# Four graph-attention layers on one core: the first unit's copies on VectorE, two additions of layer 3 by accumulating DMAs, elu's constants by GpSimd, and a new order of the work

## The chip, the core and the metric

The kernel runs on one core of a Trainium2 chip. A core has five engines with a queue each: TensorE (PE: matmuls, and PEld for its weight loads), VectorE (DVE), ScalarE (ACT), GpSimd (POOL) and SyncE (SP, which only issues DMAs here). Each works its own queue in order and waits there for semaphores. The metric is the time of one execution on the device in microseconds.

## The reference

Eight batches (B = 8) of 2048 nodes with 128 features go through four layers; all share one adjacency matrix of 2048 x 2048. Every layer is `x = x + layer(relu(layernorm(x)))`.

- Layers 0, 1 and 3 are graph attention with one head: `Wh = h W`, scores `leaky_relu(f1[i] + f2[j])`, masked by the adjacency, softmax over j, times `Wh`. Layer 0 ends with elu. Layer 3 scales its input per node, normalises `Wh` (gamma, beta), adds it again to the result, and ends with elu.
- Layer 2 is attention with four heads of 32 features, whose scores are the products of h with itself.

elu(a) is computed as `relu(a) + min(exp(a), 1) - 1`.

Cut to the end of layers 0 and 3:

```python
h_prime = jnp.einsum('bij,bjd->bid', attention, Wh)
return jax.nn.elu(h_prime)                    # layer 0
h_prime = jnp.einsum('bij,bjo->bio', attention, h) + residual
return jax.nn.elu(h_prime)                    # layer 3
```

## The kernel before, in words

**Units.** One batch in one layer is a unit, written (batch, layer) with layers 0, 1, 2, 3. `X[b]` is the batch's x, 128 partitions x 2048 columns, which stays in SBUF from its load (line 420) to the store of its two halves (line 880).

**Start of a unit.** `Unit.rows_made` normalises x: statistics on VectorE (line 451), a power on GpSimd (line 111, out `rstdx`), then the rows `h` on ScalarE (line 511), four blocks of 128 nodes per quarter. TensorE transposes a quarter (line 540). In a one-head layer (`Gat`) ScalarE copies the transposes to SBUF (`h_t`, line 558), TensorE multiplies by the weights (line 566), and `put` takes exponentials of the scores (lines 595 to 597) and writes the scaled rows `y` (line 591), all on ScalarE. `spread` makes `r`, the target's factor in all 128 partitions: for (0, 0), (0, 1) and (7, 3) by TensorE transposes (line 650) and a ScalarE copy (line 659), for others through DRAM.

**Tokens.** The attention of a one-head unit is 32 tokens: two halves of the targets times 16 blocks of sources. A token is one VectorE instruction, the front (line 718: factors `r`, `cr` and the mask `edge` into `zg`), and eight matmuls of 128 x 129 (line 727, two records each in the profile). Three `zg` buffers lie between them. There are 24 units with 32 tokens, 768 in all.

**Beats.** A unit of layer 2 is 64 beats, 512 in all. A beat is two score pairs on TensorE (line 994, two matmuls each), two exponentials on ScalarE (line 1001, 128 x 1024 each), one mask on VectorE (line 1007, 128 x 2048), and a weighing on TensorE (line 1016, four matmuls of 32 rows for one beat, mostly two beats at a time). Five `z` buffers lie between them. After 16 beats `finish` copies, transposes, divides and adds to x by an accumulating DMA from GpSimd's queue (line 1041).

**End of a half.** `out` divides the sums on VectorE into `oa` (line 760; one buffer). Layer 1 adds `oa` to x by an accumulating DMA of GpSimd (line 795). Layer 0 takes `exp` into `oe` and `relu` into `oa` on ScalarE (line 766), adds `min(oe, 1)` to x on VectorE (line 789) and `oa` by the DMA; its -1 is left out there, since layer normalisation does not see a constant. Layer 3 adds the residual `oe` (line 781), multiplies by gamma (line 783), adds beta (line 785), then `exp` and `relu`, and on VectorE line 789 and line 792, which adds `oa` and the -2 for both elus. `DIRECT` names units whose additions stay on VectorE.

**Start of the program.** SyncE issues the loads of x and of 16 adjacency rows of 1 MB (line 366); VectorE converts each to `edge` (line 369). TensorE also tests that the adjacency is symmetric (lines 382 and 386), with squares on ScalarE (line 392).

**Order.** Nothing here is ordered by hand alone. `Plan` is a planner that runs at build time: every piece of work is an `Op` with an engine, a duration, a due time, what it needs, which buffers it takes and frees, and a lag until others can see its result. `Plan.run` places at each step the op that can start first; among those that can start within `WINDOW_US` on an engine it takes the one with the earliest due time, lowered by `HURRY_US` for fronts while `zg` has more than one free buffer. The due times come from the tables `EARLY`, `TOKENS`, `BEATS` and `LEADS`. The result is a fixed order on each queue.

## Time and profile before

| | us |
|---|---|
| Median of 3 runs | 2755.65 |
| Lowest and highest | 2753.89, 2758.16 |
| Profiled execution, own time | 2748.61 |
| Its span, first to last instruction | 2746.8 |
| TensorE busy, as modelled | 2626.4 |
| VectorE busy | 2515.0 |
| ScalarE busy | 1720.2 |
| GpSimd busy | 261.7 |

A busy time is the sum over an engine's instructions; those of TensorE end where a model says so. In a list of groups, each line gives the line of the kernel, the engine, the operation, what it writes and reads, the count, the busy time, the mean duration in ns, and the idle time of the engine just before those instructions with what ended it. In a timeline a line gives start, length, engine, line and operands; brackets hold the idle time before it and what ended it.

### The profile page before, as it was taken

The page shows a single profiled execution, that of the slowest core. Times are in us where ns is not written, and L with a number is a line of the kernel's source. Part 1 is how long each engine was busy: PE and PEld are TensorE (multiplying, and loading weights), DVE is VectorE, ACT ScalarE, POOL GpSimd, SP SyncE. Part 2 cuts the span into 40 slices and gives each one's busy share as a digit, 9 for nine tenths or more (in the row PEclk, how much of TensorE's full clock was granted, in tenths as well). Part 3 has the DMA queues.
Part 4 walks back from the last instruction along what each step waited for, and adds up shares of the span by engine and source line. Part 5 has one row for each costly group of instructions (what it writes and reads, how often), then busy time and mean ns, then how long its engine had stood idle before and what let it go on. Part 6 is the DMA issues. An engine that isn't in the chain of part 4 may idle for free. (4 is left out here: it accounts for less than half of the span.)

```text
span 2746.8 us, 48941 instructions
## 1 busy us (share of the span) xinstructions
PE 2626.4 (96%) x20104; PEld 2020.1 (74%) x20104; DVE 2515.0 (92%) x3323; ACT 1720.2 (63%) x2789; POOL 261.7 (10%) x114
## 2 busy tenths in 40 slices
PE   6999999989998999999999999999999999999987
PEld 6999877757774777867777677786787667565677
DVE  7868899989999899999999999999999899899987
ACT  4333665576567558666767666665676757787651
POOL 2101010011000101111100110010111100011000
PEclk9999999999999999999999999999999999999999
DMA  8003223433323223232323321423225221422000
GB/s 311 17 9 99 64 55 62 93 85 62 62 47 77 55 55 85 55 70 55 67 62 81 78 47 47 103 53 70 55 59 105 47 58 28 108 54 55 13 16 25
DMA packets 212842, 181.80 MB, mean 66 GB/s; under 512 B 142448, under 2 KB 177728, under 8 KB 206464
## 3 DMA queue, kind: packets, MB, share of 16 engines
q1 hardware_dynamic: 144112, 156.46, 21.1%
q0 software_dynamic: 68080, 22.04, 8.0%
q8 instruction: 160, 2.62, 0.4%
q14 instruction: 74, 0.61, 0.1%
q10 hardware_dynamic: 416, 0.07, 0.0%
HBM read 123.03 MB, written 33.73 MB: 57 GB/s over the span
## 5 line engine op out<-in xcount | busy, mean ns | idle before, releaser
L1001 ACT ACTIVATE z<-ps,shift 128x1024 f32<-128x1024 f32 x1024 | 1122.7, 1113 | 727.1 <-PE ps L994 721.4
L727 PEld LDWEIGHTS ps<-y,zg 128*128 128x128 f32 x12288 | 1466.0, 192 | 71.3 <-DVE zg L718 20.0
L727 PE MATMUL ps<-y,zg 128*128 128x129 f32 x12288 | 1497.1, 276 | 15.5 <-DVE zg L718 10.4
L1007 DVE SCALAR_TENSOR_TENSOR z<-z,edge 128x2048 f32<-128x2048 f32 x512 | 1169.3, 2285 | 64.0 <-ACT z L1001 63.2
L718 DVE SCALAR_TENSOR_TENSOR zg<-r,cr,edge 128x1024 f32<-128x1024 f32 x768 | 970.5, 1278 | 98.1 <-PE ps L727 88.0
L994 PE MATMUL ps<-m,s 128*128 128x512 f32 x2048 | 721.1, 438 | 63.6 <-ACT z L1001 59.1
L994 PEld LDWEIGHTS ps<-m,s 128*128 128x128 f32 x2048 | 314.2, 191 | 339.4 <-ACT z L1001 241.1
L1016 PE MATMUL ps<-z,v 128*32 128x512 f32 x4096 | 500.9, 601 | 2.2 <-DVE z L1007 1.6
L1016 PEld LDWEIGHTS ps<-z,v 128*32 128x32 f32 x4096 | 103.5, 109 | 234.4 <-issue 183.3
L511 ACT ACTIVATE h<-x,nmrx,rstdx 128x128 f32<-128x128 f32 x512 | 210.7, 491 | 32.7 <-DVE nmrx L116 18.6
L111 POOL TENSOR_TENSOR rstdx<-varx,neg_half 128x16 f32<-128x16 f32 x31 | 130.3, 4204 | 643.9 <-DVE varx L106 643.9
L1041 POOL DMA_DIRECT2D x<-o x31 | 65.8, 2124 | 906.8 <-DVE o L1036 811.8
L451 DVE BATCH_NORM_STATS2 st<-x 128x6 f32<-128x128 f32 x496 | 106.2, 278 | 0.0
L566 PEld LDWEIGHTS ps<-rhs,h_t 128*128 128x128 f32 x768 | 98.3, 194 | 10.7 <-ACT h_t L558 3.0
L566 PE MATMUL ps<-rhs,h_t 128*128 128x130 f32 x768 | 104.3, 281 | 0.4 <-ACT h_t L558 0.3
L540 PE MATMUL ps<-ident,h 128*128 128x128 f32 x512 | 79.9, 279 | 15.7 <-ACT h L511 10.9
L795 POOL DMA_DIRECT2D x<-oa x26 | 23.4, 901 | 702.3 <-ACT z L1001 189.3
L540 PEld LDWEIGHTS ps<-ident,h 128*128 128x128 f32 x512 | 62.1, 142 | 35.0 <-ACT h L511 13.9
L760 DVE TENSOR_TENSOR oa<-ps,rs 128x384 f32<-128x384 f32 x144 | 73.9, 513 | 5.0
L558 ACT COPY h_t<-ps 128x512 f32<-128x512 f32 x96 | 55.2, 581 | 34.9 <-PE ps L540 34.9
L766 ACT ACTIVATE oe<-oa 128x1024 f32<-128x1024 f32 x32 | 33.8, 1058 | 68.8 <-DVE oa L785 59.2
L591 ACT ACTIVATE y<-ps,y 128x128 f32<-128x128 f32 x256 | 73.0, 369 | 0.0
(123 smaller groups left out, 830.7 us busy)
## 6 DMA issues: line engine op xcount, KB each, us to landing
s<-halves SPq DMA_DIRECT2D x256, 128.0 KB, 2.7
m<-halves SPq DMA_DIRECT2D x64, 512.0 KB, 6.5
r<-row SPq DMA_DIRECT2D x42, 512.0 KB, 3.7
raw<-in_adj_dram SPq DMA_DIRECT2D x16, 1024.0 KB, 16.9
x<-oa POOLq DMA_DIRECT2D x26, 512.0 KB, 4.6
values<-h SPq DMA_DIRECT2D x32, 256.0 KB, 2.2
halves<-hi SPq DMA_DIRECT2D x128, 64.0 KB, 1.7
halves<-lo SPq DMA_DIRECT2D x128, 64.0 KB, 1.7
```

The source lines that it names most:

```text
L111: nc.gpsimd.tensor_tensor(out=rstd, in0=v, in1=neg_half, op=OP.pow)
L451: nc.vector.bn_stats(out=key["st"][:, n, :], in_=rows()[:, n, :])
L511: nc.scalar.activation(self.h[q][:, k, :], X[self.b][:, n, :], AF.Relu, scale=key["rstd"][:, n:n + 1], bias=key["nmr"][:, n:n + 1])
L540: nc.tensor.transpose(pk[:, k, :], self.h[q][:, k, :], ident)
L566: nc.tensor.matmul(pv[:, k, :C + 2], lhsT=self.h_t[q][:, k * P:(k + 1) * P], rhs=rhs, start=True, stop=True)
L718: nc.vector.scalar_tensor_tensor(z, self.r[half], self.cr[:, 0, jb:jb + 1], edge[:, jb, half * HN:(half + 1) * HN], op0=OP.max, op1=OP.mult)
L727: nc.tensor.matmul(ps[:, self.banks(half, place)[i // 3], k * CE:(k + 1) * CE], lhsT=z[:, i * P:(i + 1) * P], rhs=self.y[:, jb, :], start= ...
L760: nc.vector.tensor_mul(key["a"][:, i0:i1, :], pv[:, :, :C], r[:, i0:i1, None].to_broadcast([P, i1 - i0, C]))
L994: nc.tensor.matmul(ps[:, lo + c, :], lhsT=self.S[h, jb // HB][:, at:at + P], rhs=self.M[h][:, (c2 * 2 + c) * 512:(c2 * 2 + c + 1) * 512], ...
L1001: nc.scalar.activation(self.z[s][:, c2 * HN:(c2 + 1) * HN], ps[:, lo:lo + 2, :].rearrange("p b t -> p (b t)"), AF.Exp, bias=shift)
L1007: nc.vector.scalar_tensor_tensor(self.z[s], self.z[s], 1.0, edge[:, jb, :], op0=OP.mult, op1=OP.mult, accum_out=self.den[:, h, jb:jb + 1])
L1016: nc.tensor.matmul(ps[c * HD:(c + 1) * HD, 0, :], lhsT=self.V[h][:, jb, :], rhs=z[:, c * 512:(c + 1) * 512], start=jb == 0, stop=jb == NB - 1,
```

## The change

Five things change in the code, and the planner then gives every queue a new order.

1. **First unit, (0, 0).** The four copies to `h_t` and the sixteen scaled copies to `y` (four wide multiplications now) run on VectorE. The exponentials stay on ScalarE. Fronts and the transposes of `r` need only the exponentials (`r_made`), and the first half's transposes take the PSUM bank of the sums.
2. **Layer 3, batches 0 to 6.** The addition of the residual (`L3_DMA`) and that of `oa` to x (`L3_PLUS`) become accumulating DMAs from GpSimd's queue. Batch 7 keeps both on VectorE.
3. **The constants of elu.** GpSimd subtracts 2 from x, 128 x 2048, once per batch: after the load for batches 1 to 7, for batch 0 once its first rows are made.
4. **Loads of x** for batches 1 and later wait until all adjacency rows are in. The second target tile of (0, 2) is taken through a one-element copy on GpSimd. Three small kinds of statistics buffers are now counted by the planner.
5. **The planner's numbers.** Durations, lags and all tables of due times are new.

```diff
-    HURRY_US, WINDOW_US, BEAT_SUMS_US = 70.8, 0.139, 0.86
+    HURRY_US, WINDOW_US, BEAT_SUMS_US = 38.6, 0.138, 0.86
-    EARLY = dict(front=-107.6, score=111.1, exp=-8.6, mask=-164.7, sums=-334.5)
+    EARLY = dict(front=-419.0, score=436.6, exp=-72.7, mask=-319.1, sums=-351.0)
-    DIRECT, ROWS_TURNED, L1_ACT, L3_DMA, L3_OUT = ((0, 0), (0, 1), (7, 1), (7, 2)), True, False, False, False
+    DIRECT, ROWS_TURNED, L1_ACT, L3_DMA, L3_OUT = ((0, 0), (0, 1), (7, 1), (7, 2)), True, False, True, False
+    L3_PLUS, LESS_US = True, 3.0
...
-            x_taken[b] = add("SP", 2.0, due, load, takes=["x"], lag=17.0 if b else 4.5)
+            x_taken[b] = add("SP", 0.8 if b else 2.8, due, load, loaded[:] if b else (), takes=["x"], lag=17.0 if b else 3.5)
             done[b, 0] = [x_taken[b]]
+            if b:
+                done[b, 0] = [less_two(b, due, done[b, 0])]
+
+        def less_two(b, due, needs):
+            return add("POOL", LESS_US, due + 18.0, lambda op: nc.gpsimd.tensor_scalar(
+                X[b], X[b], -2.0, None, op0=OP.add), needs)
...
+                self.less = [less_two(0, 60.0, [m[1] for m in made])] if (self.b, layer) == (0, 0) else []
...
+                    begins = (self.b, layer) == (0, 0)
...
-                        nc.scalar.copy(self.h_t[q], ps[:, turn.got["pair"], :])
+                        (nc.vector.tensor_copy if begins else nc.scalar.copy)(self.h_t[q], ps[:, turn.got["pair"], :])
...
+                    if begins:
+                        exped.append(add("ACT", 0.45, self.due(part + 0.04), lambda op, q=q, product=product:
+                                         self.put(q, product.got["pair"], False), [product] + exped[-1:]))
+                        ends.append(add("DVE", 0.75, self.due(part + 0.05), lambda op, q=q, product=product:
+                                        self.put_on_vector(q, product.got["pair"]), [exped[-1]],
+                                        frees=[("pair", product)]))
+                        continue
...
+            def put_on_vector(self, q, lo):
+                pv = ps[:, lo:lo + 2, :].rearrange("p b (k c) -> p (b k) c", c=256)
+                sl = slice(q * 4, q * 4 + 4)
+                nc.vector.tensor_mul(self.y[:, sl, :C], pv[:, :, :C], self.y[:, sl, C:CE].to_broadcast([P, 4, C]))
...
+                        room = "sums" if (self.b, self.layer, half) == (0, 0, 0) else "pair"
...
                 def elu_a(op):
-                    nc.vector.scalar_tensor_tensor(xs(), key["a"], -2.0, xs(), op0=OP.add, op1=OP.add)
+                    nc.vector.scalar_tensor_tensor(xs(), key["a"], 0.0, xs(), op0=OP.add, op1=OP.add)
...
-                last = add("DVE", 1.14, late + 4, elu_a, [last, e], frees=[("oa", taker)])
+                if L3_PLUS and b != B - 1:
+                    last = add("POOL", PLUS_US, late + 4, plus_a, [last, e], frees=[("oa", taker)], lag=PLUS_LAG_US)
+                else:
+                    last = add("DVE", 1.14, late + 4, elu_a, [last, e], frees=[("oa", taker)])
...
+                if (self.b, h) == (0, 1):
+                    def hold(op):
+                        self.M[h] = big.tile([P, N], F32R, tag="m", name="m")
+                        nc.gpsimd.tensor_copy(self.M[h][0:1, 0:1], self.M[0].bitcast(F32)[0:1, 0:1])
+                    held = add("POOL", 1.0, due, hold, self.first_target, takes=["m"])
+                    self.there, there, m_taken = there + [held], there + [held], []
...
         TOKENS = {
-            (1, 0, 0): (-22.6, 16.91), (0, 1, 0): (53.7, 14.45), (0, 1, 1): (278.3, 12.5),
+            (1, 0, 0): (-1045.4, 4.85), (0, 1, 0): (-640.7, 2.76), (0, 1, 1): (-252.6, 5.26),
...
         BEATS = {
-            (0, 0): (-186.75, 13.08), (0, 1): (-165.33, 21.31), (0, 2): (148.16, 8.98),
+            (0, 0): (-220.15, 3.75), (0, 1): (-955.77, 16.21), (0, 2): (-787.01, 14.33),
...
         LEADS = {
-            (0, 0): 491.95, (1, 0): 357.11, (0, 1): 1280.8, (2, 0): 1208.77, (1, 1): 234.77,
+            (0, 0): 213.98, (1, 0): 444.85, (0, 1): 1602.72, (2, 0): 431.88, (1, 1): 877.58,
...
```

## The prediction

> **What bounds the kernel now.** I read the page first, then the time in six windows cut at work that both versions share, then the timeline where TensorE's price per piece of work can be read, last the chain at the end.
>
> ```profile
> span 2746.8 us, 48941 instructions
> PE 2626.4 (96%) x20104; PEld 2020.1 (74%) x20104; DVE 2515.0 (92%) x3323; ACT 1720.2 (63%) x2789; POOL 261.7 (10%) x114
> ...
> L1001 ACT ACTIVATE z<-ps,shift 128x1024 f32<-128x1024 f32 x1024 | 1122.7, 1113 | 727.1 <-PE ps L994 721.4
> ...
> L1007 DVE SCALAR_TENSOR_TENSOR z<-z,edge 128x2048 f32<-128x2048 f32 x512 | 1169.3, 2285 | 64.0 <-ACT z L1001 63.2
> L718 DVE SCALAR_TENSOR_TENSOR zg<-r,cr,edge 128x1024 f32<-128x1024 f32 x768 | 970.5, 1278 | 98.1 <-PE ps L727 88.0
> ```
>
> TensorE and VectorE are both nearly full, and neither can run far ahead of the other. The busy share of TensorE is modelled, so I price its work by the distance from one start to the next:
>
> ```profile
> 2601.57 1.06 PE L1016 MATMUL ps<-z,v 128*32 128x512 f32 x8
> 2602.56 0.73 PE L994 MATMUL ps<-m,s 128*128 128x512 f32 x2
> ...
> 2604.79 1.95 PE L727 MATMUL ps<-y,zg 128*128 128x129 f32 x16
> 2606.49 0.70 PE L994 MATMUL ps<-m,s 128*128 128x512 f32 x2
> 2607.03 1.95 PE L727 MATMUL ps<-y,zg 128*128 128x129 f32 x16
> ```
>
> Token and score pair take 2607.03 - 2604.79 = 2.24 us; tokens in a row stand 1.79 apart, so a token is 1.79 and a pair 0.45 to 0.46. A weighing is 0.85 per beat plus 0.31 for each turn into the narrow form (pair and weighing, 2600.94 to 2602.56, are 1.62 = 0.46 + 0.85 + 0.31). Transposes are 0.11, projections 0.22, a symmetry matmul 0.055 per 128 columns. For the whole kernel: 768 x 1.79 + 1024 x 0.46 + 512 x 0.85 + 287 x 0.31 + 709 x 0.11 + 384 x 0.22 + about 18 = 2550 us.
>
> ```profile
> 0.00:36.00 36.00, 15.77 (x74) 11.43 (x75) 22.07 (x75) 18.98 (x60) 15.71 (x19) 1.00 0.93 365
> 36.00:88.50 52.50, 51.06 (x438) 49.59 (x439) 46.72 (x96) 15.90 (x59) 3.53 (x2) 0.97 0.45 158
> 88.50:186.70 98.20, 97.73 (x888) 93.30 (x886) 68.61 (x96) 44.09 (x127) 7.89 (x3) 1.00 0.06 17
> 186.70:2619.90 2433.20, 2360.97 (x17873) 1766.77 (x17872) 2280.35 (x2917) 1599.50 (x2448) 227.88 (x89) 1.00 0.30 64
> 2619.90:2732.10 112.20, 100.87 (x837) 98.96 (x836) 90.25 (x137) 39.60 (x96) 6.73 (x2) 0.94 0.05 15
> 2732.10:2746.80 14.70, 0.00 (x0) 0.00 (x0) 6.99 (x8) 2.11 (x2) 0.00 (x0) 0.65 0.14 41
> ```
>
> Columns: window, length, busy time of PE, PEld, DVE, ACT, POOL, granted clock, DMA share, GB/s. Stage I ends after the 64th token (186.7): 150.2 us of priced work, 36.5 idle. Stage II ends with the last weighing (2619.9): 2305.9 of work, 127.3 idle. Stage III ends with the last matmul: 93.4 of work, 18.8 idle. The tail has 14.7 us with no matmul. A change of order can only win from these 197 us.
>
> **The change, part by part.** The changed program was counted in the order in which it issues instructions on each engine. TensorE's work is the same: 2549.9, with 288 turns for 287.
>
> *Stage I.* The load of batch 1 no longer stands ahead of batch 0's: 1 MB at 365 GB/s is 2.8 us, so x and each adjacency row come that much earlier. Four copies (0.58) and sixteen scaled copies (1.14 per quarter) leave ScalarE's chain for VectorE, and the first row of r needs two quarters instead of waiting behind all four. Before, that copy ran at 33.50 and the first front at 34.52. Adding the same rows in the new order (half of x at 7.6; statistics, 1.7 of power and its end 11.6; twelve rows of h at 0.40 to 16.4; second exponentials 19.0; transposes 0.9; copy 1.0) gives r at about 21. Six edge conversions and the new copies stand before the first front in VectorE's queue, and the sixth row lands at 27.7 - 2.8 = 25, so the front comes at 26.7, 8 us earlier. Ten pairs of conversion and front follow at the pace of the rows, 2.6 us; before token 11 there is 30.4 us of TensorE work (31.5 before; symmetry now fills these gaps), and it comes at about 54 instead of 63.6: idle 24 instead of 32. Then a block of 52 statistics with their moments, 10 us without a front, stands before front 23, against two tokens in hand: 3.6 idle. GpSimd subtracts 2 from four batches here: I charge 3. Stage I: 24 + 3.6 + 3 = 31 idle, 5.5 won.
>
> *Stage II.* Fourteen additions of `oe` (1.14 apart) and fourteen of `a` go from VectorE to DMAs; in this stage 25 wide ones fewer, 28 us, and 8 fronts fewer (10 us), with 7 tokens fewer for TensorE (12 us, done in stage III). VectorE falls from about 2290 (2280 busy in the window) to 2252, TensorE from 2305.9 to 2293.7. What that is worth depends on how the work is mixed: beats need 2.2 us on VectorE and ScalarE but 1.8 to 2.1 on TensorE, tokens 1.2 against 1.79. So I took both orders four beats at a time, and summed the excess of the fullest engine over TensorE: 133 us before (the trace has 127), 115 after. Eight at a time: 78 and 71. Scaled to 127, that is 110 and 117; I take 113. In it is one bad stretch: beats 400 to 416 now have no tokens, 47 us of TensorE work against 73 of ScalarE's (32 exponentials and the rows of three units): 24 us idle at one place.
>
> The 28 extra DMAs cost 0.90 us of GpSimd each, which is 90% idle, and land 4.5 to 9.4 us after issue, median 4.6. The multiplication by gamma waits for the first one; behind it in VectorE's queue are fronts and masks. Between divide and multiplication the new order holds 4.6 to 12 us of other VectorE work, so the wait is 0 at the median and 21 us over fourteen at 9.4. I take 0, the median's value. `oa` is held longer, but the next divide is 24 us or more away, beyond what two landings (9.2) add to the usual 10 to 16.
>
> The subtraction (x, 128x2048) has no row. Least is VectorE's conversion of the same shape, 1.25; most is GpSimd's select, 0.32 for 128 columns, times 16 = 5.1. I take 3.6, the select less the 0.10 that a one-column memset takes, because engine and kind are its own. The load is hundreds of us early, so only a hold of VectorE matters. The nearest row is the power:
>
> ```profile
> 370.52 1.28 DVE L718 SCALAR_TENSOR_TENSOR zg<-r,cr,edge 128x1024 f32<-128x1024 f32 x1
> 370.75 3.84 POOL L111 TENSOR_TENSOR rstdx<-varx,neg_half 128x16 f32<-128x16 f32 x1 [1.40 <-DVE varx L106]
> ...
> 371.71 2.31 DVE L1007 SCALAR_TENSOR_TENSOR z<-z,edge 128x2048 f32<-128x2048 f32 x1
> ```
>
> The power takes 2.89 when no front runs; here it takes 3.84, as if it began when the front ended (371.80). The mask beside it loses 0.02. Ends per pass: 0.02 and 5.1. As the power reads 16 columns and then computes, I stay away from the low end, but up to three made fronts (5.4 us of TensorE work) cover a hold: 1 us per pass, 3 in stage I as said and 5 in stage II. Stage II: 113 + 5 = 118 idle, 9 won.
>
> The Trainium skill, page "SBUF — State Buffer", section "Who interferes with whom", speaks against this: a VectorE instruction with two SBUF inputs and a GpSimd one that reads SBUF lock the same port pair for a whole instruction, and the second waits. The trace shows only GpSimd as the loser. By the rule all eight passes would hold VectorE throughout, 29 us at 3.6 each, and the sum would end 21 us later.
>
> *Stage III.* From the last mask to the first token of (7, 3) the chain is 52 us long. Before, 16 tokens fill it, and five wide operations of batch 6 stand among the statistics:
>
> ```profile
> 2629.61 2.97 PE L727 MATMUL ps<-y,zg 128*128 128x129 f32 x16 [2.98 <-DVE zg L718]
> ...
> 2635.29 8.25 PE L727 MATMUL ps<-y,zg 128*128 128x129 f32 x48 [2.70 <-DVE zg L718]
> ```
>
> After, 23 tokens are left for it (41 us, with weighing and projections 49), and fronts stand among the statistics. Its idle time falls to 2, and the 4 us among the last 32 tokens stay: 6 instead of 18.8, 13 won. The tail is batch 7's, which keeps all its VectorE operations: 14.7.
>
> **The sum.** 5.5 + 9 + 13 = 27.5, so a span of 2719.3. The profiled execution took 2748.61 and the median is 2755.65, 7.0 above, so 2728.
>
> **Rivals.** *The stretch without tokens is not bought back.* Its 24 us come on top of an unchanged 127, because the page puts most of the idle on waits for exponentials, not for additions: 24 - 18.5 = 5.5 later, 2761; it is slower from 18.5 us at that place on. Against it: the count outside the stretch falls by a third. *GpSimd holds VectorE.* 5.1 us at all eight passes, all reaching TensorE: 41 - 8 = 33 on the sum, 2761; it decides from 4.4 us per pass. *The freed VectorE time counts in full.* 38 us off stage II's idle instead of 9: 2699. For it: both engines are within 1% there. *Only the end wins,* if stage I stays at the pace of the rows and stage II is as before: 2743.
>
> **How the numbers follow.** Forecast 0.50 (own range 2708 to 2740), only the end 0.16, full count 0.12, stretch 0.14, GpSimd 0.08. About 0.2% (5.5 us) is what can be told from no change. Both slower rivals lie at that bound: of their 0.22 I put 0.16 beyond and 0.06 within; of the end's 0.16, 0.03 is within. Faster 0.75, same 0.09, slower 0.16. The range from 2700 to 2763 takes in the 21 us of landings as well, and leaves out about 2 in 10.
>
> **What would show it.** First front near 27 us and the 64th token done near 181; no additions of lines 781 and 792 on VectorE before batch 7; a hole of some 24 us around beat 400; less than 4 us of TensorE waits between last weighing and first token of (7, 3); masks that stay at 2.29 us beside the subtraction. The prediction is wrong if stage II's idle is not between 95 and 140, or if multiplications by gamma wait for DMAs.

## The result, and the profile after

The changed kernel takes 2758.28 us (median of 20 executions, 2754.17 to 2765.24), the kernel before 2753.09 in the same comparison (20 executions, 2747.79 to 2760.15). The ratio is 1.0021, 95% interval 1.0014 to 1.0029: 5.2 us slower, where 27.5 us less were forecast. The profiled execution of the changed kernel took 2765.24 us, the longest of its 20; that of the kernel before took 2748.61, near the shortest of its 20. Their difference of 16.6 us overstates the change by 11, so sizes are taken from medians below, and places from the traces.

From the page of the changed kernel (part 1 and the costliest groups; the last column is the idle time before these instructions and what ended it):

```profile
span 2763.5 us, 49024 instructions
PE 2637.1 (95%) x20104; PEld 2024.9 (73%) x20104; DVE 2515.8 (91%) x3303; ACT 1712.1 (62%) x2769; POOL 331.5 (12%) x151
...
L765 PE MATMUL ps<-y,zg 128*128 128x129 f32 x12288 | 1499.2, 277 | 30.5 <-DVE zg L756 22.2
L1064 DVE SCALAR_TENSOR_TENSOR z<-z,edge 128x2048 f32<-128x2048 f32 x512 | 1170.3, 2287 | 70.4 <-ACT z L1058 67.8
L756 DVE SCALAR_TENSOR_TENSOR zg<-r,cr,edge 128x1024 f32<-128x1024 f32 x768 | 992.8, 1309 | 113.5 <-PE ps L765 97.2
```

VectorE lost 28 wide additions and is as busy as before (2515.8 against 2515.0). Part of it is in the fronts, which do the same work in 992.8 us instead of 970.5: 1309 ns on average for 1278. TensorE waits for fronts 22.2 us instead of 10.4. The timeline shows where, beside the second to eighth of GpSimd's eight passes. Here is the fifth (start, length, engine, line; "x2" is two in a row):

```profile
862.14 5.89 POOL L431 TENSOR_SCALAR x<-x 128x2048 f32<-128x2048 f32 x1 [12.77 <-DMA x<-in_x_dram]
...
862.72 5.86 DVE L756 SCALAR_TENSOR_TENSOR zg<-r,cr,edge 128x1024 f32<-128x1024 f32 x2
...
867.44 0.82 PE L765 MATMUL ps<-y,zg 128*128 128x129 f32 x5 [1.69 <-DVE zg L756]
```

Two fronts take 5.86 us there. The first has 4.67 in the trace, 3.39 more than its usual 1.28. The other passes beside fronts look the same, but for the sixth, where the front takes 3.87. At the first pass it is an edge conversion, which otherwise takes 1.23:

```profile
17.55 5.37 POOL L431 TENSOR_SCALAR x<-x 128x2048 f32<-128x2048 f32 x1 [5.17 <-DMA raw<-in_adj_dram]
17.70 6.31 DVE L371 TENSOR_SCALAR edge<-raw 128x2048 uint8<-128x2048 int32 x1
```

The excess of all VectorE instructions beside the eight passes, over their usual durations, is 28 us. The seven passes beside fronts share a pattern. Each starts while a VectorE instruction still runs and ends 5.2 us after that one's end, so first GpSimd waits and then VectorE. The held front ends 0.65 us before its pass does. Four statistics of VectorE, which read one SBUF input each, run beside the sixth pass in their usual 0.28 us; the front behind them comes later, and so is held for less (2.6 us).

The same stages as in the prediction (end of the 64th token, of the last weighing, of the last matmul; columns as there: window, length, busy time of PE, PEld, DVE, ACT, POOL, granted clock, which is the recorded share of TensorE's full clock, DMA share, GB/s):

```profile
0.00:199.70 199.70, 171.03 (x1396) 160.81 (x1396) 157.33 (x272) 73.07 (x224) 50.24 (x27) 0.95 0.32 116
199.70:2630.60 2430.90, 2354.96 (x17762) 1754.47 (x17760) 2256.11 (x2882) 1595.31 (x2440) 269.24 (x117) 1.00 0.33 69
2630.60:2748.60 118.00, 111.04 (x952) 109.62 (x948) 95.29 (x144) 41.63 (x104) 12.05 (x7) 0.97 0.18 42
2748.60:2763.50 14.90, 0.10 (x1) 0.00 (x0) 7.09 (x8) 2.11 (x2) 0.00 (x0) 0.66 0.13 40
```

With TensorE's work priced as in the prediction (150.2, 2293.7 and 106.0 us), the idle time is:

| | before | predicted | after | after, passes cut to one column |
|---|---|---|---|---|
| Stage I | 36.5 | 31 | 49.5 | 40.2 |
| Stage II | 127.3 | 118 | 137.2 | 119.7 |
| Stage III | 18.8 | 6 | 12.0 | 12.1 |
| Tail | 14.7 | 14.7 | 14.9 | 14.8 |

The last column is the first experiment below.

### The profile page after: what moved, and what is told of

Read it like the earlier page. It is cut to its first block, busy times and chain, and to the rows that moved or that the text cites. A ratio compares the mean times of both kernels' runs of the same rounds, so it can differ in the third digit from the quotient of the medians.

```text
span 2763.5 us, 49024 instructions
## 1 busy us (share of the span) xinstructions
PE 2637.1 (95%) x20104; PEld 2024.9 (73%) x20104; DVE 2515.8 (91%) x3303; ACT 1712.1 (62%) x2769; POOL 331.5 (12%) x151
## 5 line engine op out<-in xcount | busy, mean ns | idle before, releaser
L765 PE MATMUL ps<-y,zg 128*128 128x129 f32 x12288 | 1499.2, 277 | 30.5 <-DVE zg L756 22.2
L756 DVE SCALAR_TENSOR_TENSOR zg<-r,cr,edge 128x1024 f32<-128x1024 f32 x768 | 992.8, 1309 | 113.5 <-PE ps L765 97.2
L834 POOL DMA_DIRECT2D x<-oa x40 | 35.7, 892 | 934.5 <-DVE oa L798 239.6
L460 DVE BATCH_NORM_STATS2 st<-x 128x6 f32<-128x128 f32 x496 | 106.0, 282 | 1.1 <-DMA x<-oa 1.1
```

What stands on the lines that cost most here:

```text
L460: nc.vector.bn_stats(out=key["st"][:, n, :], in_=rows()[:, n, :])
L756: nc.vector.scalar_tensor_tensor(z, self.r[half], self.cr[:, 0, jb:jb + 1], edge[:, jb, half * HN:(half + 1) * HN], op0=OP.max, op1=OP.mult)
L765: nc.tensor.matmul(ps[:, self.banks(half, place)[i // 3], k * CE:(k + 1) * CE], lhsT=z[:, i * P:(i + 1) * P], rhs=self.y[:, jb, :], start= ...
```

## The experiments

Each kernel ran on one chip beside the kernel before, whose median there was 2752.1 to 2753.9 us. The table gives medians, and the ratio to the kernel before with its 95% interval. The groups of experiments ran on different chips, and differences between kernels of different groups are of medians; by the ratios, the 19.7 us below would be 18.4.

| kernel | made from | us | ratio |
|---|---|---|---|
| passes cut to one column | changed | 2738.5 | 0.9954 (0.9942 to 0.9967) |
| the first four cut | changed | 2751.2 | 0.9994 (0.9985 to 1.0002) |
| passes in sixteen pieces | changed | 2749.8 | 0.9987 (0.9977 to 0.9996) |
| subtraction by DMA | changed | 2738.4 | 0.9952 (0.9939 to 0.9965) |
| additions back on VectorE | changed | 2776.6 | 1.0087 (1.0074 to 1.0100) |
| additions by DMA, old order | before | 2788.0 | 1.0129 (1.0112 to 1.0147) |
| the same, no DMA for -2 | before | 2770.2 | 1.0059 (1.0043 to 1.0074) |
| copies back on ScalarE | subtraction by DMA | 2739.2 | 0.9951 (0.9937 to 0.9964) |
| batch 1's x early | subtraction by DMA | 2739.9 | 0.9945 (0.9932 to 0.9957) |
| the same, TensorE busier | batch 1's x early | 2736.3 | 0.9942 (0.9930 to 0.9955) |
| wide rows in the stretch | subtraction by DMA | 2740.3 | 0.9949 (0.9936 to 0.9961) |
| wide rows elsewhere | subtraction by DMA | 2740.4 | 0.9951 (0.9939 to 0.9964) |
| *on one chip:* subtraction by DMA | changed | 2742.0 | 0.9962 (0.9949 to 0.9976) |
| batch 1's x early | subtraction by DMA | 2738.8 | 0.9951 (0.9936 to 0.9965) |
| the same, TensorE busier | batch 1's x early | 2735.0 | 0.9936 (0.9922 to 0.9951) |
| the same at three places | batch 1's x early | 2734.6 | 0.9933 (0.9917 to 0.9949) |

My theory after the traces was that the passes hold VectorE and that the hold reaches the end of the program. The rivals were that other work covers it, and that the new order, with its long stretch without tokens, is what costs.

### The passes, all eight and the first four

```diff
-            return add("POOL", LESS_US, due + 18.0, lambda op: nc.gpsimd.tensor_scalar(
-                X[b], X[b], -2.0, None, op0=OP.add), needs)
+            return add("POOL", LESS_US, due + 18.0, lambda op: nc.gpsimd.tensor_scalar(
+                X[b][:, 0, 0:1], X[b][:, 0, 0:1], 0.0, None, op0=OP.add), needs)
```

The second kernel has this for batches 0 to 3 alone.

> The eight GpSimd passes over x are cut to one column each, with a constant of 0, and every instruction keeps its place; elu's constant of -2 is left out of batches' sums. Theory A (a pass holds VectorE for as long as it works, and VectorE has no slack where the first four passes lie): the wide fronts beside a pass go back from 4.66 to 1.28 us, the first front comes at about 26.7 instead of 32.2 us, the 64th token ends 13 us earlier than 199.7 (5.5 from the first pass, 7 to 8 from the next three), and each of the four late passes gives 0 to 3.4 us: 2740 to 2748 in all, about 12 to 20 below the changed kernel, so faster than the kernel before by 0.3 to 0.6%. Theory B (the passes are paid for by slack; only the first front moves): 3 to 6 us below the changed kernel, 2752 to 2755, no difference to the kernel before. Theory C (nothing hangs on the passes, the stretch without tokens is the whole cost): 2758.

> Only the passes of batches 0 to 3 are cut to one column (a constant of 0 in place of -2, which these batches' outputs then lack); those of batches 4 to 7 are whole. Theory A: first front at 26.7, 64th token some 13 us earlier than 199.7, and 11 to 14 us below the changed kernel in all (2744 to 2747). If it gains as much as the kernel with all eight cut, the four late passes cost nothing; if the difference is over 5 us, they cost as much as their hold. Theory B: 3 to 6 us. Theory C: nothing.

Measured: 2738.5 with all eight cut, 19.7 below the changed kernel; 2751.2 with the first four cut, 7.0 below. The four late passes are thus worth 12.7 us, which is what their four holds sum to in the trace (three of 3.4, one of 2.6). I had not thought that any hold would come through so completely where three fronts may be made ahead. The first four are worth 7.0, of 15.2 us of holds. No front is longer than 1.29 us in the first of these kernels. Stages of its trace:

```profile
0.00:190.40 190.40, 164.31 (x1396) 153.82 (x1396) 143.01 (x272) 73.34 (x224) 29.00 (x27) 0.98 0.33 121
190.40:2603.80 2413.40, 2347.76 (x17762) 1753.42 (x17761) 2242.86 (x2882) 1594.93 (x2440) 249.65 (x117) 1.00 0.33 70
2603.80:2721.90 118.10, 111.11 (x952) 109.61 (x948) 95.48 (x144) 41.62 (x104) 12.05 (x7) 0.97 0.18 41
```

Theory A holds, theories B and C fall. Some numbers of A missed: the first kernel is just below its 2740 to 2748 and the second above its 2744 to 2747, the first front comes at 29.4 and not at 26.7 us, and the 64th token ends 9.3 us earlier and not 13. So the early passes cost less than I expected there, and something else keeps stage I longer than before (190.4 against 186.7).

### The passes in pieces

```diff
-            return add("POOL", LESS_US, due + 18.0, lambda op: nc.gpsimd.tensor_scalar(
-                X[b], X[b], -2.0, None, op0=OP.add), needs)
+            def subtract(op):
+                for n in range(NB):
+                    nc.gpsimd.tensor_scalar(X[b][:, n, :], X[b][:, n, :], -2.0, None, op0=OP.add)
+            return add("POOL", LESS_US, due + 18.0, subtract, needs)
```

> The changed kernel, with each of the eight GpSimd passes over x (128x2048) as sixteen instructions of 128 columns in its place; same result, same order. Theory M (what holds VectorE is one GpSimd instruction at a time): a wide front beside the pieces waits for one or two of them, 1.3 to 2.0 us each in place of 4.66, the pass takes longer (6 to 12 us, as it now waits for fronts in turn), and 8 to 16 of the 19.7 us come back that the kernel with one-column passes gained: 2742 to 2750. Rival N (what counts is the total time that GpSimd works in SBUF, however it is cut): the fronts beside it lose as much in sum, 2755 to 2762.

2749.8, 8.5 below the changed kernel: theory M, at the upper end of its range. In the trace the roles are turned round at the same place (here GpSimd's line joins eight pieces):

```profile
859.47 11.32 POOL L433 TENSOR_SCALAR x<-x 128x128 f32<-128x128 f32 x8 [12.49 <-DMA x<-in_x_dram]
...
860.33 2.53 DVE L759 SCALAR_TENSOR_TENSOR zg<-r,cr,edge 128x1024 f32<-128x1024 f32 x2
862.79 2.37 DVE L1067 SCALAR_TENSOR_TENSOR z<-z,edge 128x2048 f32<-128x2048 f32 x1
```

Two fronts take 2.53 us, a mask 2.37 instead of 2.29, and the excess of all VectorE instructions beside the pieces is about 2 us in place of 28. GpSimd pays: a piece takes 0.53 us at the median and 0.97 on average, since four in ten are held up, most by a front or a mask, and a pass takes 11 to 24 us instead of 5.4 to 6.2. The three passes of batches 1 to 3 cost most: they run from 55.0 to 88.4 us, the statistics of these batches wait behind them, and the 64th token ends at 197.3, nearly as late as in the changed kernel (199.7). Stage II takes 2418.7 us, 5.3 more than with the passes cut; its trace has seven windows of half clock there against three, and whether the late pieces cost anything beside these is not shown.

The Trainium skill, page "SBUF — State Buffer", section "Who interferes with whom", states that a VectorE instruction with two SBUF inputs contends with a GpSimd instruction that reads SBUF, the shared port pair being an exclusive lock. Of VectorE's two-port modes it says that whoever issues first has the pair "for the whole instruction; the other **fully blocks** (not throttle)". The prediction weighed the rule and chose the other side. The runs agree with it on who waits, with 28 us lost beside long passes and about 2 beside short pieces. They do not show the hold to last for a whole pass: a front that ends 0.65 us before the pass and needs 1.28 was free to begin 1.9 us before the pass's recorded end.

### The subtraction by DMA

```diff
+        def constants():
+            nc.gpsimd.memset(twos, -2.0)
+            nc.scalar.dma_start(out=minus_2, in_=twos)
...
+            def subtract(op):
+                if 0 < b < B - 1:
+                    for half in range(2):
+                        nc.gpsimd.dma_start(out=X[b][:, half * HB:(half + 1) * HB, :], in_=minus_2, accum_op=OP.add)
...
-                    nc.vector.scalar_tensor_tensor(xs(), key["a"], 0.0, xs(), op0=OP.add, op1=OP.add)
+                    nc.vector.scalar_tensor_tensor(xs(), key["a"], -2.0 if b == B - 1 else 0.0, xs(), op0=OP.add, op1=OP.add)
```

Batch 0's -2 is the scalar of its own addition in layer 0.

> The whole computation, without a pass of GpSimd over x: batches 1 to 6 get their -2 by two accumulating DMAs of 512 KB from a tile of -2 in DRAM, batch 0's is the scalar of its own addition, batch 7's stays in elu on VectorE. Theory A: as with the passes cut to one column, give or take 2 us for the 6 MB of DMA in 12 transfers and some 1 us of GpSimd for each: 2740 to 2750, faster than the kernel before by 0.1 to 0.5%; the fronts beside the old places of the passes take 1.28 us. Theory C: 2758, or more if the DMAs delay other transfers.

2738.4, the same as with the passes cut, and just below the range of theory A. The whole work of the changed kernel, with the constants taken through DMAs, is 0.48% faster than the kernel before.

### The additions put back

```diff
-                    nc.gpsimd.dma_start(out=xs(), in_=key["a"], accum_op=OP.add)
+                    if layer == 3:
+                        nc.vector.tensor_add(xs(), xs(), key["a"])
+                    else:
+                        nc.gpsimd.dma_start(out=xs(), in_=key["a"], accum_op=OP.add)
...
-                        last = add("POOL", PLUS_US, due + 6, lambda op: nc.gpsimd.dma_start(
-                            out=key["a"], in_=key["e"], accum_op=OP.add), [last] + rows, lag=PLUS_LAG_US)
+                        last = add("POOL", PLUS_US, due + 6, lambda op: nc.vector.tensor_add(
+                            key["a"], key["a"], key["e"]), [last] + rows, lag=PLUS_LAG_US)
```

> Layer 3's 28 additions (14 halves, two each) that the change gave to accumulating DMAs are VectorE's again, at the same place in the order, 1.12 us each; the passes stay. If VectorE bounds and the time freed counted in full: 31 us above the changed kernel, about 2789. If it counts as my sum had it (part of the stretches bound by VectorE, part covered): 10 to 18 above, 2768 to 2776. If it lay beside other work everywhere: 0 to 3 above, 2758 to 2761, and if the transfers were late where they are used, below 2758.

2776.6, 18.3 above the changed kernel: 0.65 us for each, with 1.12 us of VectorE for an addition. That is just above the 10 to 18 of the middle theory, which my sum had used. It is not the full count, and it is not covered.

### The additions alone, in the old order

Taking them away from the kernel before should then have won as much, if the order does not matter:

```diff
-                    if k == 0:
+                    if k == 0 and b != B - 1:
+                        nc.gpsimd.dma_start(out=a, in_=key["e"], accum_op=OP.add)
+                    elif k == 0:
...
                 def elu_a(op):
+                    if b != B - 1:
+                        nc.gpsimd.dma_start(out=xs(), in_=key["a"], accum_op=OP.add)
+                        return
```

> The kernel before, in its own order, with one part of the change alone: layer 3's 28 wide additions by accumulating DMAs, each at its old place in the order. The constant -2 that one of them carried is added by two DMAs of 512 KB from a tile in DRAM ahead of layer 0's sum (batches 1 to 6) and by the scalar of an addition that is there anyway (batch 0); batch 7 is as before. No copy is moved, no pass of GpSimd, no new dues. Theory F (the freed VectorE time is worth 0.65 us per us, as putting it back cost 18.3 us for 28 additions, and it needs no new order): 2733 to 2738, 15 to 20 below the kernel before. Theory G (it is worth that only in an order planned for it; in the old one the DMAs come later than VectorE's sums did and the units behind them start late): 2748 to 2756, no difference.

2788.0, 36 us slower than the kernel before, outside all that I had expected. VectorE's statistics waited 18.2 us for x behind my own extra DMAs, so a second kernel leaves those out:

> As the kernel before with layer 3's 28 additions by DMA in the old order, but without the DMAs that add -2 ahead of layer 0's sum: the constant -2 is left out of batches 0 to 6. If the 18.2 us that VectorE's statistics waited there for x were the fault of those extra DMAs: 2762 to 2772, some 16 to 26 below that run's 2788.0, and still above the kernel before, since VectorE's multiplications by gamma wait 20 to 25 us for the first of the two DMAs. Theory F as stated there (a gain of 15 to 20 in any order) would need 2733 to 2738; theory G's no difference 2748 to 2756.

2770.2, still 16 above the kernel before. Its waits on VectorE (line waiting, what for; us in total, times, longest):

```profile
DVE zg L718 <- PE ps L727: 90.4, 130, 3.4
DVE z L1012 <- ACT z L1006: 77.2, 125, 2.8
DVE oa L785 <- DMA oa<-oe: 23.6, 7, 6.8
```

The old order has the multiplication by gamma too close behind the addition; VectorE stands in front of it until the DMA has landed. Its masks also wait longer for exponentials (77.2 us; 63.2 in the kernel before). This trace is of the shortest execution, 2761.2. In the changed kernel's order the same wait is:

```profile
DVE oa L821 <- DMA oa<-oe: 3.2, 2, 2.4
```

So theory F falls: the additions by DMA win in the new order, which leaves room for the landing, and lose in the old one, which does not. That the waits for the landing are the whole of the loss is not shown: 23.6 us of waits, less the 18.3 that the additions are worth in the new order, would make 5.3 and not 16.

### The first unit's copies

In the kernel with the subtraction by DMA, the copies of `h_t` and the scaling of `y` are ScalarE's again, each in its place:

```diff
-                        (nc.vector.tensor_copy if begins else nc.scalar.copy)(self.h_t[q], ps[:, turn.got["pair"], :])
+                        nc.scalar.copy(self.h_t[q], ps[:, turn.got["pair"], :])
...
-                nc.vector.tensor_mul(self.y[:, sl, :C], pv[:, :, :C], self.y[:, sl, C:CE].to_broadcast([P, 4, C]))
+                for k in range(4):
+                    n = q * 4 + k
+                    nc.scalar.activation(self.y[:, n, :C], pv[:, k, :C], AF.Copy, scale=self.y[:, n, C:CE])
```

> The kernel with the subtraction by DMA, with the first unit's four copies of h_t and its sixteen scalings of y on ScalarE again (each at its own place in the order; VectorE has 5.4 us less, ScalarE 8 us more). As my sum had it (every us of the first front counts): the first front comes 3 to 8 us later than 30.0 and the time is 3 to 8 us above 2738.4. Theory D: the second unit's tokens come at 124.3 whatever the first unit does, so the gap of 16.0 us in front of the 33rd front takes up the delay: the first front 3 to 8 us later, the 64th token within 1 us of 192.4, the time 2737 to 2740.

2739.2, no difference; the first front comes at 30.2 instead of 30.0 and the 64th token ends at 192.2 instead of 192.4. Both expectations were wrong on the first front: who does the copies does not set it. VectorE now stands idle for the sixth adjacency row, which must be converted ahead of the first front:

```profile
28.73 1.23 DVE L371 TENSOR_SCALAR edge<-raw 128x2048 uint8<-128x2048 int32 x1 [1.23 <-DMA raw<-in_adj_dram]
...
30.20 1.28 DVE L769 SCALAR_TENSOR_TENSOR zg<-r,cr,edge 128x1024 f32<-128x1024 f32 x1
```

The gap of theory D had nothing to take up, so this run neither supports nor harms that theory.

### The second unit's x

What keeps stage I long without the passes is visible between the 32nd and 33rd front. In the kernel with the subtraction by DMA:

```profile
108.31 1.28 DVE L767 SCALAR_TENSOR_TENSOR zg<-r,cr,edge 128x1024 f32<-128x1024 f32 x1
...
120.43 3.19 DVE L471 BATCH_NORM_STATS2 st<-x 128x6 f32<-128x128 f32 x16
...
124.33 1.28 DVE L767 SCALAR_TENSOR_TENSOR zg<-r,cr,edge 128x1024 f32<-128x1024 f32 x1
```

16.0 us without a front; the kernel before has 2.3 there. The change loads batch 1's x behind all sixteen adjacency rows. One line lets it go behind twelve:

```diff
-            x_taken[b] = add("SP", 0.8 if b else 2.8, due, load, loaded[:] if b else (), takes=["x"], lag=17.0 if b else 3.5)
+            x_taken[b] = add("SP", 0.8 if b else 2.8, due, load, loaded[:12 if b == 1 else NB] if b else (), takes=["x"], lag=17.0 if b else 3.5)
```

> The kernel with the subtraction by DMA, and batch 1's load of x waits for 12 of the 16 adjacency loads in place of all 16 (the planner then puts the first layer of batch 1 earlier, and shifts the rest). Theory D (stage I is longer than before because the second unit cannot begin: its x lands behind the whole adjacency, and the 33rd front follows the 32nd after 16.0 us, at 124.3 us, where before it followed after 2.3): that gap falls under 7 us, the 64th token ends at 181 to 185 in place of 192.4, and the whole at 2727 to 2732, 7 to 11 below 2738.4. Theory E (stage I is bound by VectorE's statistics and by the squares of the symmetry test, which stay): the gap moves but the 64th token ends at 190 to 192 and the time stays within 2 us of 2738.4.

The gap falls to 6.3 us and the 64th token ends at 184.9, 7.5 earlier, as theory D had it. But the time is 2739.9: nothing arrives at the end. Behind stage I the order of the two kernels is the same, and the trace of this one loses 11 us on the way, near 565 and 1217 us and in and behind the stretch without tokens. At each of these places the record of the granted clock has windows of 3.4 us at half of full speed: ten between the 64th token and the last weighing, against one in the kernel that it was made from.

### The stretch without tokens

From 2102.79 to 2215.92 us the changed kernel has no front, 113 us and 31 beats; the longest such stretch before is 47 us.

```profile
2102.79 1.28 DVE L756 SCALAR_TENSOR_TENSOR zg<-r,cr,edge 128x1024 f32<-128x1024 f32 x1
...
2215.92 1.28 DVE L756 SCALAR_TENSOR_TENSOR zg<-r,cr,edge 128x1024 f32<-128x1024 f32 x1 [4.75 <-DMA r<-row]
```

First, is ScalarE its bound, as the prediction said? Two kernels merge ScalarE's small instructions there, and elsewhere:

```diff
+                    if merged():
+                        n = q * 4
+                        nc.scalar.activation(self.h[q], X[self.b][:, n:n + 4, :], AF.Relu,
+                                             scale=key["rstd"][:, n:n + 1], bias=key["nmr"][:, n:n + 1])
+                        return
                     for k in range(4):
```

> The kernel with the subtraction by DMA. In the 31 beats without tokens (388 to 418 of 512), groups of four 128-column ScalarE instructions that prepare a unit (rows of h, node weights, scaling of y) are one instruction of 512 columns; the scale and bias of the second to fourth row blocks of each group are left out. 16 groups: ScalarE does some 15 us less there. Theory H (the stretch is bound by ScalarE, and nothing later gives the time back): 11 to 16 us below 2738.4, 2722 to 2727. If TensorE's 18.7 us of idle there are not ScalarE's, or the stages after it wait for something else: within 3 us of 2738.4.

> The same edit at beats 270 to 300, where tokens run beside the beats: 20 groups of four, some 18 us less work for ScalarE (the scale and bias of the second to fourth row blocks of each group are left out). Theory H: ScalarE bounds nothing there, 2735 to 2739. If ScalarE's work counts wherever it lies: some 15 to 18 us below 2738.4.

2740.3 and 2740.4, no gain in either place, so theory H falls. ScalarE has 9.2 us less to do in the stretch (94.35 busy, then 85.20; the wide instructions took 0.7 to 0.8 us and not the 0.6 I had assumed), and the stretch is 1.9 us shorter. Most of the rest went into waits for scores, first in the kernel with the subtraction by DMA, then in this one:

```profile
ACT z L1072 <- PE ps L1065: 13.7, 10, 2.9
```

```profile
ACT z L1086 <- PE ps L1078: 18.0, 16, 1.8
```

Second, does the clock matter there? In the kernel with batch 1's x early, TensorE gets more to do, of which nothing is used:

```diff
+                if 392 <= self.b * HEADS * NB + s <= 416:
+                    nc.tensor.matmul(ps[:, 2, :256], lhsT=self.S[h, jb // HB][:, at:at + P],
+                                     rhs=self.M[h][:, :256], start=True, stop=True)
```

> The kernel with batch 1's x early, and in beats 392 to 416 of the stretch without tokens TensorE does one more matmul of 256 columns ahead of each half of the scores, into a bank of PSUM that nothing uses there (50 of them, some 0.22 us each, 11 us; what they write is read by nothing). Theory K (the 7.5 us won by the 64th token are lost to half clock: in the profiled run 10 windows of 3.4 us at half clock lie between the 64th token and the last weighing, five of them between 2094 and 2197 us, against one in the kernel it was made from, because TensorE idles there): with TensorE busier the windows of half clock between 2090 and 2200 fall to 0 to 2, the stretch without fronts shrinks from 112.3 to 105 to 109 us, and the time is 3 to 8 us below 2739.9. Rival L (the stretch is a chain of scores and exponentials in which TensorE's time counts at any clock): the extra work lengthens it by 5 to 11 us, 2745 to 2751.

2736.3, 3.5 below the kernel that it was made from, with fifty matmuls more. Between 2080 and 2200 us, first without and then with them (the granted clock is the third number from the right):

```profile
2080.00:2200.00 120.00, 100.36 (x558) 49.16 (x557) 89.82 (x139) 98.15 (x160) 16.93 (x6) 0.93 0.34 62
```

```profile
2080.00:2200.00 120.00, 103.58 (x643) 56.78 (x639) 92.66 (x140) 99.23 (x163) 16.92 (x6) 0.99 0.35 62
```

The windows at half clock there fall from five to one, and the stretch without fronts shrinks from 112.3 to 109.4 us. Rival L, which needed 5 to 11 us more, falls. But these two ran on different chips, and their ratios to the kernel before hardly differ, so a second group ran on one chip, with the other two places filled as well:

```diff
-                if 392 <= self.b * HEADS * NB + s <= 416:
+                if any(lo <= self.b * HEADS * NB + s <= hi for lo, hi in ((60, 67), (202, 207), (392, 416))):
```

At the two new places the bank still holds sums that are wanted, and some of them are overwritten in this last kernel.

> The kernel with the subtraction by DMA once more: 2738 within 2 us; if the windows of half clock belong to the kernel and not to the execution, one of them again between the 64th token and the last weighing.

> Batch 1's x early once more, beside the kernel that it was made from and the one with TensorE busier, on one chip. Theory D alone (the 7.5 us of stage I reach the end): 2729 to 2732 where the kernel with the subtraction by DMA has 2738. Theory K (half clock takes them): within 2 us of that kernel, and again some 10 windows of half clock between the 64th token and the last weighing in its trace.

> TensorE busier in the stretch without tokens, once more. Theory K: 2 to 5 us below the kernel with batch 1's x early on the same chip, with 0 to 2 windows of half clock in the stretch. If the 3.5 us between them were a difference of chips: within 1 us of it.

> The same further matmuls also in beats 60 to 67 and 202 to 207 (28 more of 256 columns, some 6 us), the two other places where the trace of the kernel with batch 1's x early lost time at half clock (some 565 to 579 and 1217 us). Theory K: the windows there vanish, and 2 to 4 us come on top: 2731 to 2735. If TensorE's time counts there at any clock: 1 to 6 us above the kernel with the one stretch filled.

On one chip: 2742.0 with the subtraction by DMA (2738.0 to 2743.6), 2738.8 with batch 1's x early (2737.3 to 2743.7), 2735.0 with TensorE busier (2732.6 to 2736.2), 2734.6 with three places filled (2729.7 to 2738.3). The 3.8 us for the busier TensorE are real: no execution of the one reaches into the times of the other. The windows mostly come again in the second trace of a kernel: ten again with batch 1's x early, two with the subtraction by DMA, five with TensorE busier and none of them in the stretch. In the trace of the one with x early, the stretch is again at

```profile
2080.00:2200.00 120.00, 100.12 (x556) 47.95 (x549) 89.57 (x138) 97.52 (x159) 16.92 (x6) 0.93 0.35 62
```

Filling the other two places brought nothing more. The trace of that last kernel has windows again at 2131 and 2192 us, in the stretch and at its end, though the stretch was filled in the same way, and one at 2247; at the first of the two new places one is left of three, at the second none. It is of an execution of 2738.0 us, above the median. In this group's traces the 64th token ends about 3 us earlier with batch 1's x early, not 7.5, and the medians differ by 3.1, where the first group showed none; the ranges overlap, so that is not settled. Both traces of the kernel with x early come from its longest execution, so that the ten windows need not be in the others. So it is shown that the fifty matmuls shorten the program, and both traces of this kernel have four or five windows fewer in the stretch. That the windows are the reason is likely, but no run changes the windows alone.

The kernel with TensorE busier is the fastest that keeps the whole computation: 0.58% and 0.64% below the kernel before in the two groups.

## Why the prediction was wrong

- **The subtraction (step "stage II", third and fourth paragraph).** The step that failed. It is the one that turned a gain into a loss. Its length was taken as 3.6 us between 1.25 and 5.1; it is 5.4 to 6.2, above both ends. Its hold on VectorE was taken as 1 us per pass from the power beside a mask, 8 in all; measured are 3.4 per front (2.6 for one), 5.1 for the conversion, and 19.7 us in the median time. The power reads 16 columns, so its row could not show a hold, and I had said so and still stayed near it. Beside the four late passes the three fronts made ahead cover nothing (12.7 us of holds, 12.7 in the time): the fronts behind a held one are late as well, and VectorE, 91% busy, does not catch up. Beside the first four, half is covered. The sign that I gave, masks that stay at 2.29 us, came true all the same (2.31 at most), since the next VectorE instruction that a pass held was never a mask. It was the rival "GpSimd holds VectorE", given 0.08 and priced too high: 5.1 us at each pass, where 19.7 over eight are 2.5. Of the 30 us between 2728 and 2758.3, the passes make 11.7 (19.7 less the 8 charged). The other 18.6 lie in the terms that follow.
- **Stage I: 31 idle predicted, 49.5 found.** Cutting all passes leaves 40.2, so they cost 9 where 3 were charged. Without them 28 was predicted: 12 more. The first front is about 3 us late at 29.4. The sum had the sixth row in at 25; with the copies back on ScalarE, VectorE waits for that row until 28.73. With the passes in pieces the sixth conversion begins without a wait at 25.78 and the first front comes at 27.30, so the landing of the rows varies between these traces, and why is open. Another part is a term that the sum did not have: batch 1's load moved behind the adjacency. I counted the 2.8 us that it gave to batch 0, and never asked when the second unit can start. The 33rd front comes 16.0 us after the 32nd; loading batch 1 earlier won 7.5 us at the 64th token in one pair of traces and about 3 in another, and 0 to 3 were seen at the end.
- **Stage II: 118 predicted, 137.2 found**, inside the 95 to 140 given. The late passes make 17.5 of it in the pair of traces (12.7 in medians), where 5 were charged. Without them it is 119.7 against 113. So the count four beats at a time was right to 7 us, and the additions are worth 18.3, against 31 for a full count. (Of the two counts, 71 of 78 scaled to 127 is 116 and not 117, which does not move the 113.)
- **The wait for the first DMA: 0 predicted, 3.2 found.** Right, and for the reason given: without an order that holds other work between, it is 23.6.
- **The stretch without tokens: 24 us idle predicted at beats 400 to 416.** TensorE is idle for 23 us of the 120 from 2100 to 2220. Place and size were right, the length (31 beats, not 16) and the cause were not: with 9.2 us less for ScalarE to do, the stretch got only 1.9 shorter. So the size came out right by luck, and the two figures that it was taken from, 73 and 47, differ by 26.
- **Stage III: 6 predicted, 12 found.** The wait between the last weighing and the first token of (7, 3) is 2.5 us, under the 4 given, and 3.1 come among the last 32 tokens. Two windows at half clock (2647 to 2651 and 2688 to 2692) lose another 3.4, which the price of a token at full clock leaves out. The other 3 us are not accounted for.

In medians: the additions -18.3, the passes +19.7, and 5.2 - 19.7 + 18.3 = 3.8 for the rest of the change. This takes the parts as independent, which was not tested. With the passes cut, the traces have 7.6 us less idle time than before in stage II, 6.7 less in stage III and 3.7 more in stage I. The additions are in that, so the new order is not shown to win anything by itself. How much of the half clock is in every execution stays open, since a trace shows one of them.

## What to carry to other kernels

An engine with time to spare is not free: before work is moved to GpSimd, ask whether its instructions hold up a busy VectorE, and either keep them short (8.5 of the 19.7 us came back) or let a DMA do the work (all of it). When work goes to a DMA, the landing needs other work between it and the next user on the same queue; the same 28 transfers won 18 us in one order and cost 16 in another. When a load is moved for one unit's sake, look for the next unit that needs the one it was moved behind.

## What the runs showed of the hardware

- One GpSimd instruction over 128x2048 f32 (5.4 to 6.2 us) stops a VectorE front of two SBUF inputs for up to 3.4 us, and, the one time that they meet, a conversion of int32 to uint8, with one SBUF input, for 5.1. Statistics with one SBUF input run beside it in their usual 0.28 us. Cut into sixteen, it stops VectorE for about 2 us in sum over eight passes, and is itself stopped.
- TensorE falls to half clock without any long pause. In the stretch of the kernel with batch 1's x early it is busy for 100 of 120 us, no gap is over 1.9 us with ends as the profile models them, and five windows of 3.4 us are at half. With fifty useless matmuls, four or five of these were gone and the program was 3.8 us shorter; with 28 more of them elsewhere the median was the same, and the one trace has a window in the stretch again. I had not expected extra work on the fullest engine to pay. The kernel with the subtraction by DMA has gaps of the same sum there (20.3 us against 19.6) and one window, so the sum alone does not decide; what does stays open.
